# Last stage of a two-layer kernel: the value products move ahead of the score products in three slots of four, and two other steps move with them

## The chip, the cores and the metric

The kernel runs on one NeuronCore of a Trainium2 chip, all in fp32. The metric is the device time of one execution in microseconds. Engines are called as in the profile: PE is TensorE (its matmuls; PEld are its weight loads), DVE is VectorE, ACT is ScalarE, POOL is GpSimd, SP is the engine that issues most DMAs.

## What is computed

The input `x` has 16 batch elements of 256 tokens with 256 features. Four layers add to it one after another: a cross-attention, a top-2 mixture of experts, a second cross-attention, and a gated linear attention. The change is in the last one. For each of 8 heads of 64 features it computes (cut to what matters):

```
q1, k1, v  = x@Wq, x@Wk, x@Wv                  # dense part
q2         = x@Wqa@Wqb ;  k2 = softmax(x@Wka@Wkb)   # routed part
gk1, gk2   = log_sigmoid(x@Wg1a@Wg1b + b)/16, log_sigmoid(x@Wg2a@Wg2b + b)/16
S_t = diag(exp(gk_t)) S_{t-1} + k_t^T v_t ;  o_t = q_t S_t     # for (q1,k1,gk1)
o  += the same with (q2,k2,gk2), each token kept by the one expert it is routed to
o   = o * rsqrt(mean(o*o) + eps) * norm_w
o   = o * (g * sigmoid(g)),   g = x@Wga@Wgb
x  += tanh(gate) * (o @ Wo)
```

## The kernel before, in words

The kernel writes the recurrence as causal scores over all 256 tokens. With c the running sum of the log gates, `q*exp(c)` and `k*exp(-c)` are multiplied to a table tokens x tokens, masked, and applied to `v`. There are two such tables for each head, the first for the dense part and the second for the routed part. They are added before they meet `v`.

**Slots.** The last stage (`stage3_fast`, L1619) runs over 64 slots, `for p in range(last)`, with p = 4b + m: batch element b, and m = 0..3 a pair of heads. Small steps of the coming batch elements (projections, gates, routing, norms) are hung into the slots by lists (`middle`, `rest`, `late`, `behind_mask`, `by_rows`, `logs`, from L2039), each with the slot number m in which it runs. Every engine is pinned to the order of the program (`Pinned`, L42): an instruction that waits holds up all that is behind it on its engine. So the order of the calls in the loop is the order on each engine.

**The steps of a slot before**, with the names of the tiles that the profile shows:

- `masked(p - 1, 1)`: four DVE operations multiply the second scores of the slot before with the routing table `am` and with 1/denominator (`at<-sc,kden,am`); POOL then adds the result to the first scores (`at<-at,at`).
- `keys_queries(p + 1)`: the projections of the next slot's keys and queries (`kq`, PE).
- The hung-in steps. In m = 0 `lows` (`low`: small projections, copied by DVE). In m = 1 `all_gates` (the gates `sc<-lbg,low` and `z<-lbg,low`, of which ACT takes the exponential, `lg`), then the mean squares of the outputs (`ms`). In m = 2 the values (`v`, copied by ACT). In m = 3 the output projection (`proj`, added to `x` by DVE). On DVE there are also reductions of the gates (`gates`), the routing tables (`em`, `am`) and the routing itself.
- `decays(p + 1)`: running sums of the log gates as a product with a triangular matrix (`gq<-dmask,lg`, `gz<-em,lg`), and their exponentials on ACT (`ee`).
- `products(p, 0)`: the first scores (`sc<-f`). `masked(p, 0)`: one DVE operation applies the causal mask (`at<-sc,amask`).
- In m = 0 `route_logits`: `emx` and `e` on DVE, `e<-e` (an exponential) on ACT.
- `factors(p + 1)`: one DVE operation, `f<-kq,ee`.
- In m = 0 `outgates`: the output gate (`zg`, two banks); ACT takes an exponential (`eg<-zg`), and DVE a copy (`zs<-zg`).
- `summed(p)`: `values(p - 1)`, that is `o<-at,v`, and after each second slot the squares (`sq<-o`, ACT).
- `second(p + 1)`: `gq<-low,lbk` and `gz<-low,lbk` (queries and later keys of the routed part). `factors_second(p + 1)`: POOL makes `k`, DVE makes `q`.
- The list `logs`, where in m = 1 the statistics of `x` for a later norm stand: `stats(b + 2)`, two BNStats and two aggregates on DVE (`bst`, `mv`) and four small POOL operations (`rs`).
- `products(p, 1)`: the second scores (`sc<-q,k`).
- At the start of m = 0 also `shares` and `shares_end`: the softmax denominators of the routed keys (`den`, then `dens` on DVE).

**PSUM.** Of the eight banks, four are fixed (`kq`, `gq`, `gz`, `o`), two form the one tile `sc` (pool `psa`, one buffer), and two are general (pool `pss`, two buffers in turn, called by `bank(...)`). The tile `sc` holds the first scores, then the second scores, and in m = 1 a part of the gates. Each of these writers waits until the last reader of the one before is done. The general banks take `den`, `low`, `zg`, `z`, `ms`, `v` and `proj`.

**Shapes on PE.** A product with 128 rows and 128 columns fills the array. `sc`, `zg` and `gq/gz<-low` use halves of it (64 rows x 128 columns, two at a time), `o` uses 128 rows x 64 columns, `den` and `ms` 128 x 32, the gates 17 rows. An fp32 matmul shows as two passes in the trace: "x8" is four matmuls.

Of the kernel before, what the change touches and what calls it, by code (L numbers as in the profile page):

```python
# [10 lines left out]
F32 = mybir.dt.float32  # L11
# [6 lines left out]
P = 128  # L18
B, S, D = 16, 256, 256
# [7 lines left out]
def bc(ap, shape, *axes):  # L27

    for a in axes:
        ap = ap.unsqueeze(a)  # L30
    return ap.to_broadcast(list(shape))
# [42 lines left out]
def layers(ctx: ExitStack, tc: tile.TileContext, t, out, check):  # L74
# [102 lines left out]
    dve3, act3, pool3 = free = [Pinned(tc, x, False) for x in (nc.vector, nc.scalar, nc.gpsimd)]  # L177
# [371 lines left out]
    if fast:  # L549
        route = Route()  # L550
# [319 lines left out]
    weights = []  # L870
# [748 lines left out]
    def stage3_fast(early_bank):  # L1619

        with ExitStack() as sx:
# [7 lines left out]
            def bank(name):  # L1629
                return pss.tile([P, 512], F32, tag="ps", name=name) if pss else early_bank(name)  # L1630

            def tokens(i):
                return slice(i * P, (i + 1) * P)


            def matmul(*a, **k):
                tc.keep_in_program_order(nc.tensor.matmul(*a, **k))  # L1637
# [41 lines left out]
            def turn(b):  # L1679
                xnT[b] = of(b).tile([P, 2, S], F32, tag="xnT", name="xnT")  # L1680
                ps = bank("tr")
                for k in range(2):
                    for i in range(2):
                        transpose(ps[:, (2 * k + i) * P:(2 * k + i + 1) * P], xn[b][:, i, k * P:(k + 1) * P], ident)
                act3.copy(xnT[b], ps.rearrange("p (k s) -> p k s", k=2))
# [28 lines left out]
            e_, den_, z_, rl, rows, cols_ = {}, {}, {}, {}, {}, {}  # L1714
# [121 lines left out]
            def place(p):  # L1836
                b, m = p // 4, p % 4
                return b, m, slice(m * P, (m + 1) * P)
# [37 lines left out]

            def shares(b):

                ps = bank("den")
                x = e2[b].rearrange("p m (i q t) -> p (m i) q t", i=2, q=4)  # L1880
                for q in range(4):
                    matmul(ps[32 * q:32 * q + 32, :S], halves[:, 48:80], x[:, :, q, :], start=True, stop=True)
                z_[b, "den"] = ps
# [11 lines left out]
            def factors(p):  # L1895
                fk[p, 0] = w2.tile([P, 2, S], F32, tag="f0", name="f0")
                dve3.tensor_tensor(fk[p, 0], kq.pop(p).rearrange("p (w s) -> p w s", w=2), ee.pop((p, 0)),
                                        ALU.mult)
                fq[p, 0] = fk[p, 0][:, 1, :]
                fk[p, 0] = fk[p, 0][:, 0, :]  # L1900
# [9 lines left out]
            def products(p, n):  # L1910

                b, m, cols = place(p)
                q, k = fq.pop((p, n)), fk.pop((p, n))
                ps = psa.tile([P, 2, 512], F32, tag="sc", name="sc")
                for lo, hi, i in ((0, S, 0), (P, S, 1)):
                    for j in range(2):
                        r = slice(64 * j, 64 * j + 64)
                        matmul(ps[:, j, lo + i * P:hi + i * P], k[r, tokens(i)], q[r, lo:hi],
                                         start=True, stop=True)
                z_[p, n, "sc"] = ps  # L1920

            def masked(p, n):
                b, m, cols = place(p)
                ps = z_.pop((p, n, "sc"))
                a = w2.tile([P, 2, 384], F32, tag=f"at{n}", name=f"at{n}")
                if n == 0:
                    at[p] = a
                    dve3.tensor_tensor(a, ps[:, :, :384], bc(amask, [P, 2, 384], 1), ALU.mult)
                else:
                    r = rd[b][:, 2 * m:2 * m + 2, :]  # L1930
                    for lo, hi, i in ((0, S, 0), (S, 3 * P, 1)):
                        for j in range(2):
                            dve3.scalar_tensor_tensor(a[:, j, lo:hi], ps[:, j, lo:hi], r[:, i, j:j + 1],
                                                           am[b][:, lo:hi], ALU.mult, ALU.mult)
                    if p == last - 1:
                        at[p] = a
                        return
                    pool3.tensor_tensor(at[p], at[p], a, ALU.add)

            def values(p, first=True, end=True):  # L1940
                b, m, cols = place(p)
                if m % 2 == 0:
                    o[b, m // 2] = psu.tile([P, 512], F32, tag="o", name="o")
                ps, a = o[b, m // 2], at[p] if not end else at.pop(p)
                base = m % 2 * S
                for i, (lo, hi, to) in enumerate(((0, S, base), (S, 3 * P, base + P))):
                    for j in range(2):
                        h = slice((2 * m + j) * 64, (2 * m + j + 1) * 64)
                        matmul(ps[64 * j:64 * j + 64, to:base + S], v[b][:, i, h], a[:, j, lo:hi],
                                         start=first and i == 0, stop=end and i == 1)  # L1950
# [4 lines left out]
            def squares(b, mp):  # L1955
                if mp == 0:
                    u_[b] = w2.tile([P, 4, S], F32, tag="u", name="u")
                    oT[b] = u_[b]
                    sq[b] = w2.tile([P, 4, S], F32, tag="sq", name="sq")
                ps = o.pop((b, mp))  # L1960
                act3.activation(sq[b][:, 2 * mp:2 * mp + 2, :].rearrange("p m s -> p (m s)"), ps, AF.Square)
                z_[b, mp, "o"] = ps

            def gated(b, mp):
                ps = z_.pop((b, mp, "o"))
                dve3.tensor_tensor(u_[b][:, 2 * mp:2 * mp + 2, :].rearrange("p m s -> p (m s)"), ps,
                                        gw[b][:, 2 * mp:2 * mp + 2, :].rearrange("p m s -> p (m s)"), ALU.mult)
# [63 lines left out]
            def warm():  # L2031

                ps = bank("warm")
                for _ in range(2):
# [3 lines left out]
            start = {3: [(same, 1)]}  # L2038
            middle = {0: [(lows, 1)], 1: [(outgates_end, 0, 0), (all_gates, 1)], 3: [(scaled_first, 0)]}  # L2039

            rest = {0: [(bias, 2)], 1: [(route_sums, 1)], 2: [(norm_ahead, 2), (steepest, 1, 0)], 3: [(steepest, 1, 1), (weights, 1)]}
            late = {1: [(norms, -1)], 2: [(vals, 1), (turn_ahead, 2)], 3: [(project, -1)]}
            behind_mask = {0: [(route_logits, 1)]}
            by_rows = {0: [(outgates, 0)], 1: [(gates_end, 1)]}
            logs = {0: [(outgates_exp, 0, 1, act3.copy)],
                    1: [(route, 1), (stats, 2), (outgates_end, 0, 1), (gate_logs, 1, 0)],
                    2: [(gate_logs, 1, 1), (normed_out, -1, 0), (normed_out, -1, 1)]}

            def run(steps, p):
                for f, d, *a in steps.get(p % 4, ()):  # L2050
                    if 0 <= p // 4 + d < B:
                        f(p // 4 + d, *a)
# [17 lines left out]
            psa = sx.enter_context(tc.tile_pool(name="f3psa", bufs=1, space=PSUM, reuse_waits="tile"))  # L2070
            pss = sx.enter_context(tc.tile_pool(name="f3ps", bufs=2, space=PSUM, reuse_waits="tile"))
            last = 4 * B
            decays(0)
            for m in range(0, 3, 2):
                ps = bank("k2")
# [7 lines left out]
            def summed(p):  # L2083
                values(p - 1)
                if p % 2 == 0:
                    squares((p - 1) // 4, (p - 1) % 4 // 2)

            for p in range(last):
                if p == 0:
                    turn(1)  # L2090
                run(start, p)
                if p % 4 == 0:
                    shares(p // 4)
                if 0 < p:
                    masked(p - 1, 1)
                if p % 4 == 0:
                    shares_end(p // 4)
                if 1 < p and p % 2 == 1:
                    gated((p - 2) // 4, (p - 2) % 4 // 2)
                if p + 1 < last:  # L2100
                    keys_queries(p + 1)
                run(middle, p)
                run(rest, p)
                if p + 1 < last:
                    decays(p + 1)
                run(late, p)
                products(p, 0)
                masked(p, 0)
                run(behind_mask, p)
                if p + 1 < last:  # L2110
                    factors(p + 1)
                run(by_rows, p)

                inside = 0 < p and p + 1 < last
                if inside:
                    summed(p)
                if p + 1 < last:
                    second(p + 1)
                    factors_second(p + 1)
                run(logs, p)  # L2120
                products(p, 1)
                if 0 < p and not inside:
                    summed(p)

            b, p = B - 1, last - 1
            values(p, end=False)
            masked(p, 1)
            project_part(b, 0, 0)
            values(p, first=False)
# [122 lines left out]
```

## Time and profile before

| | us |
|---|---|
| three timed runs | 1804.23, 1805.36, 1807.59; median 1805.36 |
| the profiled execution | 1804.92 |
| its span in the profile | 1803.0 |
| PE busy | 1771.7 (98%) |
| DVE busy | 1168.2 (65%) |
| POOL busy | 1018.9 (57%) |
| ACT busy | 842.4 (47%) |
| granted PE clock, mean | 0.997 |

The 64 slots lie between 1221 and about 1785 us. A line of the timeline gives the start and the length in us, the engine, the line of the kernel (L1637 is the matmul helper of this stage, L50 the helper of the other engines), the operation, the tile written and the tiles read, shapes, and how many instructions were merged; in brackets stands the idle time of the engine before it and what ended it. Lines in a group list have the busy time and the mean length in ns, then the idle time before. Matmuls are pipelined: the length of one (0.38 us for a 256-column pass) is longer than the distance of two starts (0.22 us), so distances of starts are what counts on PE.

### The profile page before, as it was taken

How to read it: one execution, taken by the hardware profiler on the slowest of the kernel's cores; microseconds unless marked ns; L12 is line 12 of the kernel's file. 1: busy time of each engine (PE TensorE's matmuls, PEld its weight loads, DVE VectorE, ACT ScalarE, POOL GpSimd, SP SyncE). 2: the span in 40 equal slices, each digit the busy share in tenths (PEclk: the TensorE clock that was granted, in tenths of full speed). 3: DMA queues.
4: the chain of work that ended last, by engine and by line, in shares of the span. 5: the costliest groups of instructions: out<-in, count | busy, mean ns of one | idle time of the engine just before them, and what ended most of it. 6: DMA issues, size and time to landing. Idle time of an engine off the chain costs nothing.

```text
span 1803.0 us, 35245 instructions
## 1 busy us (share of the span) xinstructions
PE 1771.7 (98%) x13802; PEld 1227.0 (68%) x13802; DVE 1168.2 (65%) x2727; ACT 842.4 (47%) x1743; POOL 1018.9 (57%) x1002
## 2 busy tenths in 40 slices
PE   8999999999999999999999999999999999999997
PEld 5666666667666666667677866656777777777775
DVE  3345666666656656665566368886777777777774
ACT  4433444334444345344343368765455455545542
POOL 3655776576756766566751776513545455544543
PEclk9999999999999999999999999999999999999999
DMA  9800010000100010000037952200112111211210
GB/s 304 238 1 23 16 36 13 28 17 13 35 26 17 17 33 10 28 24 17 13 126 250 272 122 47 43 4 18 35 35 51 44 35 41 46 41 35 51 38 26
DMA packets 121623, 102.28 MB, mean 57 GB/s; under 512 B 53051, under 2 KB 106979, under 8 KB 120937
## 3 DMA queue, kind: packets, MB, share of 16 engines
q1 hardware_dynamic: 109161, 83.17, 16.0%
q0 software_dynamic: 12288, 16.79, 4.6%
q8 instruction: 110, 1.80, 0.4%
q14 instruction: 64, 0.52, 0.1%
HBM read 56.26 MB, written 38.44 MB: 53 GB/s over the span
## 4 chain that ended last, share of the span: by engine, by line
PE 83%; POOL 7%; DVE 5%; issue 1%; ACT 1%; DMA 1%; SPq 0%; POOLq 0%; DVEq 0%; ACTq 0%
PE o L50 12%; PE qk L50 11%; PE v L50 9%; PE sc L50 8%; PE proj L50 7%; PE kq L1637 6%; PE sc L1637 6%; PE gq L1637 4%; POOL es L50 4%; PE o L1637 3%; PE ex L50 3%; PE proj L1637 3%; PE v L1637 3%; PE gz L1637 2%; POOL rs L50 2%; PE low L1637 2%
## 5 line engine op out<-in xcount | busy, mean ns | idle before, releaser
L50 POOL TENSOR_SCALAR rs<-mv 128x2 f32<-128x2 f32 (+2 forms) x85 | 16.3, 192 | 398.3 <-DVE mv L50 393.7
L50 POOL TENSOR_TENSOR at<-at,at 128x768 f32<-128x768 f32 x63 | 114.3, 1814 | 184.0 <-DVE at L50 184.0
L50 DVE RECIPROCAL rd<-o 128x256 f32<-128x256 f32 x64 | 112.3, 1755 | 155.8 <-PE o L50 155.8
L50 ACT ACTIVATE e<-sc 128x1024 f32<-128x1024 f32 (+1 forms) x192 | 181.6, 1016 | 18.4 <-PE sc L50 18.4
L50 PE MATMUL sc<-qk 64*128 64x256 f32 (+1 forms) x1536 | 183.1, 384 | 0.5 <-DVE qk L50 0.5
L50 PE MATMUL o<-e,v 128*32 128x256 f32 (+1 forms) x3072 | 177.9, 379 | 0.0
L50 PEld LDWEIGHTS sc<-qk 64*128 64x128 f32 (+1 forms) x1536 | 132.0, 172 | 55.1 <-issue 26.8
L50 POOL TENSOR_TENSOR esum<-esum,es 128x512 f32<-128x512 f32 x128 | 163.5, 1277 | 10.0
L50 PE MATMUL qk<-kvT,wkv 128*128 128x333 f32 x512 | 164.3, 443 | 0.0
L50 POOL TENSOR_TENSOR es<-e 128x1024 f32<-128x1024 f32 x64 | 151.3, 2364 | 12.1 <-ACT e L50 9.0
L50 ACT ACTIVATE qk<-qk 128x256 f32<-128x256 f32 x128 | 48.8, 381 | 231.5 <-PE qk L50 231.5
L50 POOL TENSOR_TENSOR es<-es,e 77x1024 f32<-77x1024 f32 x64 | 150.5, 2351 | 5.0
L50 PEld LDWEIGHTS o<-e,v 128*32 128x32 f32 (+1 forms) x3072 | 99.9, 110 | 66.3
L50 PE MATMUL qk<-kvT,wq 128*128 128x256 f32 x512 | 134.6, 385 | 0.0
L50 DVE COPY qk<-qk 128x333 f32<-128x333 f32 x128 | 64.6, 505 | 94.8 <-ACT qk L50 93.3
L50 POOL DMA_INDIRECT x<-rows_out,pos x64 | 100.9, 1577 | 35.5 <-issue 16.6
L50 PEld LDWEIGHTS qk<-kvT,wq 128*128 128x128 f32 x512 | 94.3, 189 | 35.1 <-issue 9.6
L50 PEld LDWEIGHTS qk<-kvT,wkv 128*128 128x128 f32 x512 | 97.2, 190 | 30.0
L50 DVE TENSOR_TENSOR at<-sc,amask 128x768 f32<-128x768 f32 x64 | 61.3, 957 | 84.9 <-PE sc L1637 83.9
L50 PE MATMUL proj<-wo0h,oT 128*128 128x256 f32 x512 | 113.7, 380 | 0.3 <-DVE oT L50 0.3
L50 PE MATMUL v<-wkv,kvT 128*128 128x512 f32 x256 | 113.1, 595 | 0.0
L50 PEld LDWEIGHTS proj<-wo0h,oT 128*128 128x128 f32 x512 | 95.9, 190 | 13.9 <-issue 0.8
(259 smaller groups left out, 3912.5 us busy)
## 6 DMA issues: line engine op xcount, KB each, us to landing
rows<-zero SPq DMA_DIRECT2D x16, 640.0 KB
xin<-rows SPq DMA_DIRECT2D x16, 640.0 KB
r<-rms SPq DMA_DIRECT2D x30, 256.0 KB
rows_out<-y SPq DMA_DIRECT2D x16, 384.0 KB
v<-vctx SPq DMA_DIRECT2D x15, 308.0 KB
x<-in_x_dram SPq DMA_DIRECT2D x16, 256.0 KB
rows_out<-y SPq DMA_DIRECT2D x16, 256.0 KB
rows<-picks SPq DMA_DIRECT2D x16, 256.0 KB
```

The lines of the kernel that those rows point to most:

```text
L50: x = getattr(self.engine, name)(*a, **k)
L1637: tc.keep_in_program_order(nc.tensor.matmul(*a, **k))
```

## The change

Four things are moved, and no arithmetic is changed.

1. In slots with m = 0, 2, 3 (`ahead`), `factors(p + 1)` and `summed(p)`, so `o<-at,v`, run before `products(p, 0)` in place of after it. The first slot moves only `factors`, the last one nothing; m = 1 stays as it was.
2. In slots with m = 2 and 3 the second scores go to two general banks (`sc1`), in place of the tile `sc`. In exchange `den` goes from a general bank to the tile `sc`.
3. The four mask operations of the second scores run head by head, in place of block by block.
4. `stats(b + 2)` moves within m = 1 from the list `logs` to the list `rest`: before the first scores, their mask and `k`, in place of after them.

```diff
 def shares(b):
-    ps = bank("den")
+    ps = psa.tile([P, 2, 512], F32, tag="sc", name="den")[:, 0, :]
...
 def products(p, n):
-    ps = psa.tile([P, 2, 512], F32, tag="sc", name="sc")
+    if n == 1 and m > 1:
+        two = [bank("sc1"), bank("sc1")]
+    else:
+        ps = z_[p, n, "sc"] = psa.tile([P, 2, 512], F32, tag="sc", name="sc")
+        two = [ps[:, 0, :], ps[:, 1, :]]
     for lo, hi, i in ((0, S, 0), (P, S, 1)):
         for j in range(2):
             r = slice(64 * j, 64 * j + 64)
-            matmul(ps[:, j, lo + i * P:hi + i * P], k[r, tokens(i)], q[r, lo:hi],
+            matmul(two[j][:, lo + i * P:hi + i * P], k[r, tokens(i)], q[r, lo:hi],
                              start=True, stop=True)
-    z_[p, n, "sc"] = ps
+    if n == 1:
+        z_[p, n, "sc"] = two
...
 def masked(p, n):
-        for lo, hi, i in ((0, S, 0), (S, 3 * P, 1)):
-            for j in range(2):
-                dve3.scalar_tensor_tensor(a[:, j, lo:hi], ps[:, j, lo:hi], r[:, i, j:j + 1],
+        for j in range(2):
+            for lo, hi, i in ((0, S, 0), (S, 3 * P, 1)):
+                dve3.scalar_tensor_tensor(a[:, j, lo:hi], ps[j][:, lo:hi], r[:, i, j:j + 1],
                                                am[b][:, lo:hi], ALU.mult, ALU.mult)
...
-rest = {0: [(bias, 2)], 1: [(route_sums, 1)], 2: ...
+rest = {0: [(bias, 2)], 1: [(route_sums, 1), (stats, 2)], 2: ...
...
-        1: [(route, 1), (stats, 2), (outgates_end, 0, 1), (gate_logs, 1, 0)],
+        1: [(route, 1), (outgates_end, 0, 1), (gate_logs, 1, 0)],
...
     run(late, p)
+    inside = 0 < p and p + 1 < last
+    ahead = p % 4 != 1 and p + 1 < last
+    if ahead:
+        factors(p + 1)
+        if inside:
+            summed(p)
     products(p, 0)
     masked(p, 0)
     run(behind_mask, p)
-    if p + 1 < last:
+    if not ahead and p + 1 < last:
         factors(p + 1)
     run(by_rows, p)
-
-    inside = 0 < p and p + 1 < last
-    if inside:
+    if inside and not ahead:
         summed(p)
```

More of the change, by code (lines that the diff above doesn't have):

```diff
@@ L2039, in stage3_fast @@
             middle = {0: [(lows, 1)], 1: [(outgates_end, 0, 0), (all_gates, 1)], 3: [(scaled_first, 0)]}
-            rest = {0: [(bias, 2)], 1: [(route_sums, 1)], 2: [(norm_ahead, 2), (steepest, 1, 0)], 3: [(steepest, 1, 1), (weights, 1)]}
+            rest = {0: [(bias, 2)], 1: [(route_sums, 1), (stats, 2)], 2: [(norm_ahead, 2), (steepest, 1, 0)], 3: [(steepest, 1, 1), (weights, 1)]}
             late = {1: [(norms, -1)], 2: [(vals, 1), (turn_ahead, 2)], 3: [(project, -1)]}
```

## The prediction

> **What bounds the kernel now.** I read the page first, then stretches of the last stage (1221 to 1795 us) in the timeline, engine by engine.
>
> ```profile
> span 1803.0 us, 35245 instructions
> ## 1 busy us (share of the span) xinstructions
> PE 1771.7 (98%) x13802; PEld 1227.0 (68%) x13802; DVE 1168.2 (65%) x2727; ACT 842.4 (47%) x1743; POOL 1018.9 (57%) x1002
> ...
> PE 83%; POOL 7%; DVE 5%; issue 1%; ACT 1%; DMA 1%; SPq 0%; POOLq 0%; DVEq 0%; ACTq 0%
> ```
>
> TensorE (PE) is the bound. In the last stage the starts of its matmuls show how strictly: from one `kq` to the next, slots take 9.78, 8.35, 7.64 and 9.19 us, the same to 0.01 us from batch to batch with two exceptions (slots 36 and 46). A batch takes 34.96 us, and nearly all of it is issued without a pause. So little waiting is there to be removed, and the question is which chains beside PE are just as long. One is. I number slots p = 4b + m. This is p = 40 (m = 0); first PE, then VectorE (DVE), then ScalarE (ACT):
>
> ```profile
> 1586.73 0.92 PE L1637 MATMUL sc<-f 64*128 64x256 f32 x8
> ...
> 1592.46 0.70 PE L1637 MATMUL sc<-lbg,low 17*128 17x512 f32 x2
> ```
>
> ```profile
> 1587.77 0.96 DVE L50 TENSOR_TENSOR at<-sc,amask 128x768 f32<-128x768 f32 x1 [0.53 <-PE sc L1637]
> 1588.76 0.18 DVE L50 TENSOR_REDUCE emx<-rl 32x8 f32<-32x32 f32 x1
> 1588.97 0.18 DVE L50 TENSOR_TENSOR e<-rl,emx 32x32 f32<-32x32 f32 x1
> 1589.18 0.69 DVE L50 TENSOR_TENSOR f<-kq,ee 128x512 f32<-128x512 f32 x1
> 1590.07 0.69 DVE L50 COPY zs<-zg 128x512 f32<-128x512 f32 x1 [0.19 <-ACT eg L50]
> 1590.67 0.41 DVE L50 TENSOR_TENSOR q<-gq,ee 128x256 f32<-128x256 f32 x1
> 1591.00 1.38 DVE L50 SCALAR_TENSOR_TENSOR at<-sc,kden,am 128x256 f32<-128x256 f32 x4
> ```
>
> ```profile
> 1589.19 0.23 ACT L50 ACTIVATE e<-e 32x32 f32<-32x32 f32 x1 [1.58 <-DVE e L50]
> 1589.43 0.60 ACT L50 ACTIVATE eg<-zg 128x512 f32<-128x512 f32 x1
> ```
>
> Read it as a chain. The first score group `sc<-f` ends; its mask starts 1.04 us after the group's start; `e` on DVE releases `e` on ACT; that lets `eg` run; `zs` starts 0.03 us after `eg` ends; then `q`, then the second mask, which ends at 1592.39. The gate matmuls of slot p = 41 (`sc<-lbg,low`) write the same `sc` tile and start at 1592.46. PE gets there by its own work at 1592.46 too. From `sc<-f` to the gates both paths are 5.73 us long. That there is no slack is seen at p = 44, where the mask came 0.35 us later relative to its slot:
>
> ```profile
> 1623.08 0.96 DVE L50 TENSOR_TENSOR at<-sc,amask 128x768 f32<-128x768 f32 x1 [0.88 <-POOL k L50]
> ```
>
> ```profile
> 1627.76 0.70 PE L1637 MATMUL sc<-lbg,low 17*128 17x512 f32 x2 [0.27 <-DVE at L50]
> ```
>
> The gates came 0.34 us later in their slot, and PE is shown waiting for DVE. Delay on this chain is delay of the kernel.
>
> **The change, part by part.**
>
> *Values ahead of the scores.* The eight passes `o<-at,v` (128 rows x 64 columns) stand between `sc<-f` and `gq/gz<-low` (both 64 rows x 128 columns); in slots m = 0, 2, 3 they move ahead of `sc<-f` (not in the first and the last slot). Each change of the array's shape costs: `sc<-f` takes 0.85 us to the next start if `o` follows and 0.75 if the equally shaped `zg` does; the first `gq` pass after `o` takes 0.32 us, against 0.22 in slot 0, where no `o` stands before it (1239.75 to 1239.97). One stay in the 64-row shape is saved in each slot: 0.10 + 0.10 = 0.20 us. Before `o` the array comes from another shape as before, so that side stays. `o` needs the sum `at` of the slot before from GpSimd (POOL): in slot 40 it is ready at 1585.08 and `o` moves to 1586.73; in slots 2 and 3 there are about 1.5 us as well, once the statistics are out of the way. No cost.
>
> *Slots m = 2 (16 of them).* -0.20 us. The second scores go to two general banks, last used by `v`, whose second copy ends at 1605.31, 1.1 us before the scores would come (1606.42). Nothing waits.
>
> *Slots m = 3.* -0.20 us, but a wait is added: `den` moves from a general bank to the `sc` tile, so it waits for the first mask. What that takes is in the last slot, where nothing else stands between:
>
> ```profile
> 1780.68 0.92 PE L1637 MATMUL sc<-f 64*128 64x256 f32 x8
> 1782.74 0.49 PE L1637 MATMUL sc<-q,k 64*128 64x256 f32 x2 [1.13 <-DVE at L50]
> ```
>
> 2.05 us from `sc<-f` to the next writer of the tile. In slot 3 PE will have 0.75 (`sc<-f`) + 0.43 (`gq/gz` without the switch) + 0.75 (`sc<-q,k`) = 1.93 us of work, so `den` waits 0.12, and all PE work behind it (`kq`, `low`) with it. DVE is free in time: the projection's sum ends at 1579.54, `factors` takes 0.68, the mask is due about 1580.3. Bounds of this wait: 0 to 0.4 (if the masks `em`, which wait for a DMA, come late). I take 0.12.
>
> *Slots m = 0 (p = 4 to 56: 14 with the chain).* The -0.20 is still PE's, but `sc<-f` starts 0.80 us later, behind `o` (its row: 1588.45 to 1589.25). The whole chain above hangs on it. `factors` leaves the place between `e` and `zs`, but there it lay beside `e` and `eg` on ACT (it ended at 1589.87, `eg` at 1590.03), so its absence shortens nothing. At its new place it waits only for `ee` (1587.05) and is done by 1588.0, before the mask at 1588.57. So mask, `e`, `eg`, `zs`, `q` and second mask each come 0.80 later, and the gates start at 1593.26 in place of 1592.46. PE will reach them at about 1592.3 and idle 1.0 us. Queued behind them are `gq`, `gz`, `ms` and the next `sc<-f`; that one already waits for ACT to empty the gates (2.78 us after them), so nothing is caught up in m = 1. Net +0.80 us from `kq` to the gates, the 0.20 swallowed.
>
> Here a rule weighs. The Trainium skill, *PSUM — Partial Sum Buffer*, "PSUM bank collisions raise a hardware error", says that two engines must not be in one bank and quadrant at once, two readers included, and that the scheduler therefore adds a dependency between them. `eg` and `zs` read one bank, and the row has `zs` 0.03 us behind `eg`. If that were only a coincidence of order, `zs` could start straight after `e`, with `factors` gone, about 0.9 us sooner: the second mask would end where it does now and the slot would cost nothing. By the rule and the row it can't; I take +0.80.
>
> *Statistics sooner (m = 1).* Two BNStats and two aggregates, about 0.97 us of DVE (1599.51 to 1600.48), move ahead of the mask, where DVE now idles from 1593.42 to 1596.28; they fit even if held up behind POOL's 1.81 us sum. On POOL the four small `rs` steps (1.56 us) move ahead of `k`, needed a slot later. This is what frees the sum `at` of m = 1, now done at 1605.14 while the moved `o` of m = 2 wants it at 1604.43: without it 0.7 us would be lost per batch. On its own it gives nothing. Its DMAs: SP still waits for `picks` before `rows` and `cols`, and `turned` follows those; nothing moves.
>
> *Mask order and squares.* Four masks per slot either way, 1.38 us. `squares` goes ahead of `e` on ACT, which idles there 1.58 us and needs 0.59. Nothing.
>
> *The end.* In slot 63 the second scores no longer wait for the mask, only for the projection's bank (emptied at 1781.54): 1781.6 in place of 1782.74, -1.1 us, and the tail behind follows. Slots 58 to 60, after the last gates, give -0.20 - 0.08 - 0.20 = -0.5; in slot 62 the projection waits for POOL's `u` anyway.
>
> **Sum.** Per batch -0.20 - 0.20 + 0.12 + 0.80 = +0.52 us; x14 = +7.3. Less 1.1 and 0.5 at the end, and 0.3 for the accident of slot 44, which lies off the new path: +5.4 us. On the profiled execution (1804.9 us, span 1803.0) that is 1810.3. The median of the three timed runs is 1805.36, 0.4 above it; I predict 1810.6 us.
>
> **Rivals.**
> - *The chain has slack after all, and the change is faster.* If the gates are not moved by the late mask (a slack of 0.80 us or more in m = 0 would be needed), slot 0 gives -0.20 too: 14 x -0.48 = -6.7, with -1.6 at the end -8.3 us: 1797. For it: the 0.20 us per switch is plain in the rows, at three places a batch. Against it: p = 44.
> - *About half of the shift arrives*, because something of the chain is overlapped (`zs` or `q` sooner): +0.1 per batch, 1805 to 1806, no change that can be told.
> - *More waits than I see*: `den` at its upper bound (+0.3 a batch), or masks held up behind POOL steps as at p = 44 (+0.35 in m = 1, where the slack for `sc<-q,k` is only 0.14). +0.4 to 0.6 a batch: 1816 to 1819.
> - *The change does not do what it says.* Freeing the second scores from the first mask is worth nothing in the middle: waits of `sc<-q,k` for DVE sum to 1.5 us over slots 1257 to 1757 us. This is already in the sum.
>
> **How the numbers follow.** About 0.2% (3.6 us) can be told from no change. The likeliest case, 1807 to 1814, has 0.60, of which 0.08 lies below 1809. More waits 0.13, half the shift 0.12, the chain with slack 0.15. Slower: 0.52 + 0.13 = 0.65; same 0.08 + 0.12 = 0.20; faster 0.15. The range 1802 to 1818 takes in the likeliest case, the half shift and most of the added waits, and leaves out the faster rival.
>
> **What would show it.** From one `kq` to the next, the four slots of a batch are now 8.35 (m = 0), 7.64 (m = 1), 9.19 (m = 2) and 9.78 us (m = 3); by the sum they become 8.15, 8.64, 8.99 and 9.70, 35.5 in all. In m = 1 the gates should stand 1.0 us behind the end of PE's `kq`, with DVE's second mask named as what ended the wait; in m = 0 the mask should start 0.80 us later in its slot with `zs` still 0.03 us behind `eg`; in m = 3 `den` should start 2.05 us after `sc<-f`. I am wrong if the gates follow `kq` without a wait, if `zs` starts before `eg` ends, or if PE waits in m = 2.

## The result, and the profile after

The changed kernel takes 1816.98 us (median of 4 runs, 1814.86 to 1817.81), the kernel before 1805.54 us on the same chips. The ratio is 1.0066 [1.0053, 1.0079]: slower by 11.4 us; the brackets hold the 95% interval of the ratio. The profiled execution took 1814.86 us, the fastest of the four. From its page:

```profile
span 1813.1 us, 35294 instructions
## 1 busy us (share of the span) xinstructions
PE 1765.4 (97%) x13802; PEld 1227.1 (68%) x13802; DVE 1164.8 (64%) x2727; ACT 845.4 (47%) x1743; POOL 1019.9 (56%) x1002
...
PE 79%; DVE 7%; POOL 7%; ACT 3%; issue 2%; DMA 1%; SPq 0%; POOLq 0%; DVEq 0%; ACTq 0%
```

TensorE is busy 6.3 us less in a span that is 10.1 us longer: it does the same instructions and stands still more. In the chain that ended last its share falls from 83 to 79%, and VectorE's and ScalarE's rise from 5 and 1% to 7 and 3%. The list of waits, asked for PE over the fourteen full batches of the last stage, says where (waited for, us in total, times, longest us); first after, then before:

```profile
PE sc L1637 <- DVE at L50: 13.1, 14, 0.9
PE o L1637 <- POOL at L50: 1.3, 1, 1.3
PE den L1637 <- DVE at L50: 0.5, 1, 0.5
PE proj L1637 <- DVE at L50: 0.5, 2, 0.2
```

```profile
PE sc L1637 <- DVE at L50: 1.7, 3, 1.2
```

One wait a batch of 0.94 us has come, always the same: a matmul into the tile `sc` that waits for a mask on DVE. (Waits under 0.15 us are not in this list.) The timeline of PE in slot p = 40 (m = 0) shows which matmul:

```profile
1592.86 0.87 PE L1637 MATMUL o<-at,v 128*64 128x256 f32 x8
1593.66 0.92 PE L1637 MATMUL sc<-f 64*128 64x256 f32 x8
...
1596.56 1.13 PE L1637 MATMUL kq<-xnT,wk 128*128 128x256 f32 x4
1597.53 1.03 PE L1637 MATMUL kq<-xnT,wq 128*128 128x256 f32 x4
1599.49 0.70 PE L1637 MATMUL sc<-lbg,low 17*128 17x512 f32 x2 [0.94 <-DVE at L50]
```

It is the gates of slot 41. Without a wait they follow the start of `kq<-xnT,wq` by about 0.97 us; here by 1.96. The same slot on DVE, then on ACT:

```profile
1593.40 0.69 DVE L50 TENSOR_TENSOR f<-kq,ee 128x512 f32<-128x512 f32 x1
1594.70 0.96 DVE L50 TENSOR_TENSOR at<-sc,amask 128x768 f32<-128x768 f32 x1 [0.61 <-PE sc L1637]
1595.69 0.18 DVE L50 TENSOR_REDUCE emx<-rl 32x8 f32<-32x32 f32 x1
1595.90 0.18 DVE L50 TENSOR_TENSOR e<-rl,emx 32x32 f32<-32x32 f32 x1
1596.99 0.69 DVE L50 COPY zs<-zg 128x512 f32<-128x512 f32 x1 [0.91 <-ACT eg L50]
1597.72 0.42 DVE L50 TENSOR_TENSOR q<-gq,ee 128x256 f32<-128x256 f32 x1
1598.06 1.38 DVE L50 SCALAR_TENSOR_TENSOR at<-sc,kden,am 128x256 f32<-128x256 f32 x4
```

```profile
1593.77 0.60 ACT L50 ACTIVATE sq<-o 128x512 f32<-128x512 f32 x1
1596.12 0.23 ACT L50 ACTIVATE e<-e 32x32 f32<-32x32 f32 x1 [1.74 <-DVE e L50]
1596.37 0.60 ACT L50 ACTIVATE eg<-zg 128x512 f32<-128x512 f32 x1
```

The chain is the one of before, link by link, only later. DVE stands idle for 0.91 us ahead of `zs`, which starts 0.02 us after `eg` ends; the second mask ends at 1599.44, and PE goes on at 1599.49. Meanwhile the squares and the new place of the factors, both done by 1594.4, have shortened nothing.

Measured from one `kq` to the next, the slots of a batch are:

| slot | before | predicted | after |
|---|---|---|---|
| m = 0 | 8.35 | 8.15 | 8.25 |
| m = 1 (holds the gates' wait) | 7.64 | 8.64 | 8.65 |
| m = 2 | 9.19 | 8.99 | 8.99 |
| m = 3 | 9.78 | 9.70 | 9.79 |
| batch | 34.96 | 35.5 | 35.68 |

14 x 0.72 = 10.1 us, the whole difference of the spans. The other terms nearly cancel (they are in the section on the prediction).

### The profile page after: what moved, and what is told of

Same layout as the page of the kernel before. It is cut to its first block, busy times and chain, and to the rows that moved or that the text cites. A ratio compares the mean times of both kernels' runs of the same rounds, so it can differ in the third digit from the quotient of the medians.

```text
span 1813.1 us, 35294 instructions
## 1 busy us (share of the span) xinstructions
PE 1765.4 (97%) x13802; PEld 1227.1 (68%) x13802; DVE 1164.8 (64%) x2727; ACT 845.4 (47%) x1743; POOL 1019.9 (56%) x1002
## 4 chain that ended last, share of the span: by engine, by line
PE 79%; DVE 7%; POOL 7%; ACT 3%; issue 2%; DMA 1%; SPq 0%; POOLq 0%; DVEq 0%; ACTq 0%
PE o L50 12%; PE qk L50 11%; PE v L50 9%; PE sc L50 8%; PE proj L50 7%; PE sc L1637 5%; PE kq L1637 5%; POOL es L50 4%; PE ex L50 3%; PE proj L1637 3%; PE o L1637 3%; PE gq L1637 3%; PE v L1637 2%; DVE at L50 2%; POOL rs L50 2%
## 5 line engine op out<-in xcount | busy, mean ns | idle before, releaser
L50 POOL TENSOR_TENSOR at<-at,at 128x768 f32<-128x768 f32 x63 | 114.4, 1816 | 224.5 <-DVE at L50 224.5
```

What stands on the lines that cost most here:

```text
L50: x = getattr(self.engine, name)(*a, **k)
```

## The experiments

The theory: the loss is the m = 0 chain, and only there; its stiff link is that `zs` on DVE waits for `eg` on ACT, and `eg` for the routing's exponential. Rivals: the moved steps themselves (factors, statistics), the general banks or the wait of `den` cost the time; or the values ahead give nothing anywhere. Each ratio below is to the kernel before, timed in the same rounds on the same chip, with its 95% interval in brackets. Each diff is against the changed kernel, unless the text names another; `...` stands for lines left out.

**Values ahead in m = 2 and 3 only.**

```diff
-ahead = p % 4 != 1 and p + 1 < last
+ahead = p % 4 > 1 and p + 1 < last
```

> The changed kernel, with the values ahead of the first scores in slots m = 2 and 3 alone (m = 0 as before the change). Theory 1 (the loss is the chain of slot m = 0: mask, e, eg, zs, q, second mask, gates): from kq to kq 8.35 (m = 0), 7.64, 8.99, 9.79 us, the gates follow kq without a wait; a batch 34.8 us, and with the shorter last slot some 4 us less than the kernel before. Rival (the loss is den's new wait and the second scores in general banks): still 5 us or more above the kernel before.

Measured: 1804.11 us, ratio 0.9995 [0.9987, 1.0003]. The slots are 8.35, 7.65, 8.99 and 9.79. The loss is gone with the moved values of m = 0. The slots are as expected, but the 4 us did not come: the interval takes in no change at all. From the last `kq` to the end it takes 32.75 us, as in the kernel before (32.77), where 1.1 us less was expected. More on the end, and on m = 3, which gives nothing, follows below.

**Values ahead in m = 0 only.**

```diff
-ahead = p % 4 != 1 and p + 1 < last
+ahead = p % 4 == 0 and p + 1 < last
```

> The changed kernel with the values ahead in slots m = 0 alone. Theory 1: the gates come 0.91 us later in 14 batches, nothing is saved in m = 2 and 3 and den does not wait: 14 x 0.91 - 1.1 = 11 to 12 us above the kernel before, no better than the whole change. Rival: m = 0 saves its 0.20 us in each batch and den no longer waits: 2 to 4 us under the kernel before.

Measured: 1817.18 us, 1.0070 [1.0056, 1.0084]; slots 8.25, 8.65, 9.19 and 9.78. This slot alone makes the whole loss.

**No values ahead; the other parts stay.**

```diff
-ahead = p % 4 != 1 and p + 1 < last
+ahead = False
```

> The changed kernel without its first part: values and factors behind the first scores in all slots; general banks for the second scores, den in the tile sc, head by head masks and earlier statistics stay. Theory 1: slots as in the kernel before (den has 2.7 us behind sc<-f and does not wait), 1.1 us less in the last slot: 1 us under the kernel before. Rival (den, banks or statistics carry the loss): 5 to 10 us above it.

Measured: 1803.88 us, 0.9995 [0.9987, 1.0003]. All four slots are as before to 0.01 us. The second scores in other banks, the masks head by head and the statistics sooner, taken together, cost nothing and give nothing in the middle by themselves; they were not run one by one.

**The stiff link cut.** ACT's exponential of the routing goes behind `eg`, so that `eg`, and with it `zs`, no longer hangs on `e` from DVE.

```diff
-    act.activation(e, e, AF.Exp)
+def route_exp(b):
+    act.activation(e_[b], e_[b], AF.Exp)
...
-by_rows = {0: [(outgates, 0)], 1: [(gates_end, 1)]}
+by_rows = {0: [(outgates, 0), (route_exp, 1)], 1: [(gates_end, 1)]}
... (and the same step ahead of the loop, for the first batch element)
```

> The changed kernel with one step more moved: in slot m = 0 ScalarE takes the routing exponential e behind eg, the first exponential of the output gate, in place of ahead of it. All the values stay ahead. Theory 1: eg no longer hangs on the mask, zs starts right after e on VectorE, about 0.9 us sooner, and the gates come at 10.3 us after kq (11.18 in the changed kernel, 10.27 in the one before); 14 x 0.88 = 12 us less than the changed kernel, about level with the kernel before or 1 us under it. Rival (den, banks): nothing changes, 10 us or more above the kernel before.

Measured: 1802.89 us, 0.9989 [0.9981, 0.9997]: 14 us less than the changed kernel with one small step of 0.23 us moved (12.0 by the spans of the profiled executions, as expected). The same slot, p = 40, on DVE, then ACT, then PE:

```profile
1586.98 0.96 DVE L50 TENSOR_TENSOR at<-sc,amask 128x768 f32<-128x768 f32 x1 [0.61 <-PE sc L1637]
1587.97 0.18 DVE L50 TENSOR_REDUCE emx<-rl 32x8 f32<-32x32 f32 x1
1588.18 0.18 DVE L50 TENSOR_TENSOR e<-rl,emx 32x32 f32<-32x32 f32 x1
1588.41 0.69 DVE L50 COPY zs<-zg 128x512 f32<-128x512 f32 x1
1589.14 0.42 DVE L50 TENSOR_TENSOR q<-gq,ee 128x256 f32<-128x256 f32 x1
1589.48 1.38 DVE L50 SCALAR_TENSOR_TENSOR at<-sc,kden,am 128x256 f32<-128x256 f32 x4
```

```profile
1587.79 0.60 ACT L50 ACTIVATE eg<-zg 128x512 f32<-128x512 f32 x1 [1.13 <-PE zg L1637]
1588.41 0.23 ACT L50 ACTIVATE e<-e 32x32 f32<-32x32 f32 x1
```

```profile
1589.82 1.03 PE L1637 MATMUL kq<-xnT,wq 128*128 128x256 f32 x4
1590.92 0.70 PE L1637 MATMUL sc<-lbg,low 17*128 17x512 f32 x2
```

ACT's wait ahead of `eg` is now for PE's `zg` and no longer for DVE, and `zs` needs to wait no more; from the first mask's start to the second's it is 2.50 us in place of 3.36. The first mask is as late as in the changed kernel, and yet the gates come only 0.13 us behind PE's own pace. The late mask alone does not make the loss; it takes the link as well.

**The same cut in the kernel before.** Its edit is the one above, on the kernel before.

> The kernel before with one step moved: e's exponential behind eg on ScalarE in slot m = 0. It shortens the chain from the first scores to the gates by about 0.8 us, while TensorE's own way there stays 5.73 us long. Theory 1 (both ways are equally long before, TensorE is the bound): no change beyond 0.5 us. Rival (the chain already holds TensorE up before the change): up to 0.8 x 14 = 11 us faster.

Measured: 1805.39 us, 0.9999 [0.9990, 1.0008]. DVE's second mask, then PE's gates, in slot 40:

```profile
1593.26 1.38 DVE L50 SCALAR_TENSOR_TENSOR at<-sc,kden,am 128x256 f32<-128x256 f32 x4
```

```profile
1594.03 1.03 PE L1637 MATMUL kq<-xnT,wq 128*128 128x256 f32 x4
1594.99 0.70 PE L1637 MATMUL sc<-lbg,low 17*128 17x512 f32 x2
```

The mask is done at 1594.64, 0.35 us before the gates, and they come no sooner: before the change the two paths were equally long, so shortening one is worth nothing.

**Factors back behind the first mask.** The values stay ahead.

```diff
-if ahead:
-    factors(p + 1)
-    if inside:
-        summed(p)
+if ahead and inside:
+    summed(p)
...
-if not ahead and p + 1 < last:
+if p + 1 < last:
     factors(p + 1)
```

> The changed kernel with factors back behind the first mask in all slots; values stay ahead. In the changed kernel the gates are 0.91 us late in slot m = 0, 0.80 of it the later mask, and 0.11 because q on VectorE starts 0.72 us after zs, where it started 0.61 after it before. Theory A: the 0.11 comes with the place of factors (it no longer stands between e and zs): q starts 0.61 behind zs again, 1.5 us less than the changed kernel. Theory B: it comes with something else of the later mask: q stays at 0.72, no change to the changed kernel. Either way the first part keeps its loss without factors: 9 us or more above the kernel before.

Measured: 1825.1 us, 1.0107 [1.0092, 1.0123], 8 us more than the changed kernel. One thing came as theory A has it: in m = 0 the second mask starts 9.62 us after `kq`, not 9.74. I missed the total: the tile `kq` has one buffer, and PE now waits for the factors that read it. PE in a slot m = 2:

```profile
1620.32 0.82 PE L1637 MATMUL sc<-q,k 64*128 64x256 f32 x8
1621.87 1.10 PE L1637 MATMUL kq<-xnT,wk 128*128 128x256 f32 x4 [0.73 <-DVE f L50]
```

The slot is 9.79 in place of 8.99. Where the values go ahead, the mask and all that follows it come late, and the factors must leave its back. This part of the change, which I had costed at nothing, is a condition of the first.

**Statistics back behind the second scores.**

```diff
-1: [(route_sums, 1), (stats, 2)]
+1: [(route_sums, 1)]
...
-1: [(route, 1), (outgates_end, 0, 1), (gate_logs, 1, 0)]
+1: [(route, 1), (stats, 2), (outgates_end, 0, 1), (gate_logs, 1, 0)]
```

> The changed kernel with the statistics back at their old place in slot m = 1. By the prediction the sum at of m = 1 is then ready 0.7 to 0.8 us after the moved values of m = 2 want it: slot m = 2 grows from 8.99 to 9.7 or 9.8 us, 15 x 0.75 = 11 us above the changed kernel (about 1828). If the place of the statistics doesn't matter: equal to the changed kernel.

Measured: 1825.95 us, 1.0116 [1.0101, 1.0132]. PE in a slot m = 2:

```profile
1615.55 3.60 PE L1637 MATMUL v<-wv,xnT 128*128 128x512 f32 x8
1619.84 0.87 PE L1637 MATMUL o<-at,v 128*64 128x256 f32 x8 [0.69 <-POOL at L50]
```

```profile
1615.22 0.19 POOL L50 TENSOR_SCALAR rs<-mv 128x2 f32<-128x2 f32 x1 [3.75 <-DVE mv L50]
...
1617.97 1.82 POOL L50 TENSOR_TENSOR at<-at,at 128x768 f32<-128x768 f32 x1
```

The moved values wait for GpSimd's sum, which stands behind the statistics' steps there and ends at 1619.79; the slot is 9.75 in place of 8.99. The 0.7 us a batch of the prediction is 0.76.

**The cut, and values ahead in m = 0 and 2 only.** The edit of the cut, and:

```diff
-ahead = p % 4 != 1 and p + 1 < last
+ahead = p % 4 in (0, 2) and p + 1 < last
```

> The version with e's exponential behind eg, with the values ahead in slots m = 0 and 2 alone (in m = 3 as before the change). If den's wait (0.21 us) eats what m = 3 saves (0.20), and the values ahead there make late routing masks em cost more, this is equal to or up to 1.5 us faster than that version with m = 3 too: about 1801.5, 4 us under the kernel before. From kq to kq 8.25, 7.79, 8.99, 9.78. If m = 3 did save something, it is 2 to 3 us slower than that version.

Measured: 1803.44 us, 0.9986 [0.9979, 0.9992]; slots 8.25, 7.79, 8.99 and 9.78. It is no slower without the values ahead in m = 3, so these give nothing. Nor do those of m = 0, even with the cut: 8.25 + 7.79 is 0.05 more than the 8.35 + 7.64 of before.

**Values ahead in m = 2 only, and not in slot 62.** This came from comparing the ends of the kernels above.

```diff
-ahead = p % 4 != 1 and p + 1 < last
+ahead = p % 4 == 2 and p + 2 < last
```

> Values ahead of the scores only in the slots m = 2, and not in slot 62; the rest of the change stays. Theory: the array change saves 0.20 us in m = 2 and nothing elsewhere, so the four slots of a batch are 8.35, 7.64, 8.99 and 9.78 us, 34.76 in all, 0.20 less than before, 14 times: -2.8. In the changed kernel the moved values of slot 62 wait 0.64 us for GpSimd's sum, and the whole stretch from the last kq to the end is 32.87 us; with the values back it is 32.1, as in the kernel with no values ahead (before: 32.77): -0.7. In all -3.5 us, about 1802.0. Rival: the tail loses its gain to the second scores in a general bank alone; then the stretch stays near 32.8 us and the time is about 1802.7. If the slots m = 2 had gained only through their neighbours, they would stay at 9.19 and the time at about 1804.8.

Measured: 1800.78 us (8 runs), 0.9974 [0.9964, 0.9985], the fastest of all, and faster than both kernels. The slots are 8.35, 7.65, 8.99 and 9.78, as expected; the last `kq` to the end takes 32.23 us (32.1 expected, 32.87 in the changed kernel). In slot 62 of the changed kernel PE reads:

```profile
1783.71 0.87 PE L1637 MATMUL o<-at,v 128*64 128x256 f32 x8 [0.64 <-POOL at L50]
...
1787.64 1.10 PE L1637 MATMUL ms<-sq,halves 128*128 128x512 f32 x2 [1.12 <-DVE at L50]
```

The first wait goes with this edit, the second stays (0.93 us in the kernel with no values ahead): `ms` wants a general bank, and the second scores now hold one until their mask is done. Before, `ms` did not wait.

**`den` back in a general bank,** with values ahead in m = 2 and 3 but not in slot 62.

```diff
-ps = psa.tile([P, 2, 512], F32, tag="sc", name="den")[:, 0, :]
+ps = bank("den")
...
-ahead = p % 4 != 1 and p + 1 < last
+ahead = p % 4 > 1 and p + 2 < last
```

> Values ahead in the slots m = 2 and m = 3 (not in slot 62), and the denominator den back in a general bank, where it does not wait for the first mask; the rest of the change stays. Theory: the slots m = 3 gain nothing in the changed kernel because den waits 0.21 us for the mask, so without that wait they are 9.58 us in place of 9.79, den starts about 1.93 us after sc<-f, and a batch is 8.35 + 7.64 + 8.99 + 9.58 = 34.56 us: -5.6 us over 14 batches and -0.7 at the end, about 1799.2. Rival: the restart of PE behind a semaphore, not the mask, sets the place of den, and it stays near 2.14 us with the slot at 9.79: about 1802.2. If the general banks run short, because the second scores and den now both want them, a wait appears at den or behind it, and the slot is longer than 9.79.

Measured: 1817.99 us, 1.0064 [1.0051, 1.0078]. It did not tell theory and rival apart; the third case came. PE, then DVE, in a slot m = 3:

```profile
1588.70 0.82 PE L1637 MATMUL sc<-q,k 64*128 64x256 f32 x8
1590.64 0.64 PE L1637 MATMUL den<-e,halves 128*32 128x256 f32 x8 [1.11 <-DVE at L50]
```

```profile
1589.76 1.38 DVE L50 SCALAR_TENSOR_TENSOR at<-sc,kden,am 128x256 f32<-128x256 f32 x4
```

The general banks are short: `den` waits for the first head's half of the second mask (it ends at 1590.49) in place of the first mask, and the slot is 10.77 us. The move of `den` into `sc` belongs to the move of the second scores out of it.

## Why the prediction was right, and where its sizes were wrong

The direction, the place and the mechanism were right: the m = 0 chain has no slack, a mask 0.80 us late moves the gates, and the wait stands in m = 1 where it was forecast. The size was off, +11.4 us by the medians in place of +5.2. It lies in the stated range, but not in the likeliest case (1807 to 1814): it is where the rival "more waits than I see" had its 1816 to 1819. By the profiled executions, cut at the `kq` of slots 2, 58 and 61:

| term | predicted | measured |
|---|---|---|
| up to slot 2 | 0 | -0.3 |
| 14 batches, regular | +7.3 | +10.1 |
| accidents in them | -0.3 | +0.3 |
| slots 58 to 60 | -0.5 | -0.2 |
| the end | -1.1 | +0.1 |
| sum | +5.4 | +10.0 |

Of the 4.6 us that were missing, 1.5 are 0.11 a batch in m = 0, 1.3 are 0.09 a batch at `den`, 1.2 the end and 0.6 the accidents; the rest cancels. So the range held, but the sum reached only half of the loss.

*m = 2, -0.20.* Right to 0.01 us, and the runs show that the move gives it: with the values ahead the slot is 8.99, without 9.19, in every kernel in which PE does not wait there. That a change of shape is what it saves is read from the rows.

*m = 0, +0.80.* Too small by 0.11. Each step down to `zs` came later by 0.80 exactly, then `q` follows `zs` by 0.72 us, before by 0.61, so the gates come 11.18 us after `kq` in place of 10.27. "Its absence shortens nothing" was said of the factors; their absence costs 0.11: with them back behind the mask, the second mask came 0.12 sooner. What matters is the step on DVE before `zs`. Where that is the routing's `e`, which works on partitions 64 to 95 only, `q` starts 0.03 us after `zs` ends. Where it is `factors`, or the first mask as in slot 60 (which has no routing step), both on all 128 partitions, `q` starts 0.08 us before `zs` ends. This is so in all twelve profiles, wherever PE does not hold `q` up. The runs show the order that costs the 0.11, not the reason.

The saving of 0.20 was only 0.10 in the slot itself (`sc<-q,k` takes 0.85 us to `kq` in place of 0.75), which the gates' wait swallows. The other 0.10 goes into a wait that I had not looked for. In m = 0 the second scores still need the tile `sc`. Before, they came 1.05 us after the first mask's end; now they start 0.05 us after it (1595.71 after 1595.66). The loads of their weights, before and after:

```profile
1589.57 0.84 PEld L1637 LDWEIGHTS sc<-q,k 64*128 64x128 f32 x8
```

```profile
1595.71 0.73 PEld L1637 LDWEIGHTS sc<-q,k 64*128 64x128 f32 x8 [0.23 <-DVE at L50]
```

Before, the load ran 0.21 us ahead of the first pass (1589.78); now it starts with it, and that pass takes 0.32 us to the next in place of 0.22. This is the same 0.10 as at `gq` behind `o`, where the load also starts with the pass (1589.25), but here the shape of the array does not change. So the rows tie this 0.10 to weights that are not loaded ahead; a change of shape is one case of it.

The step that made me take +0.80 holds as far as it was used: `zs` waits for `eg`. In the slot above it starts 0.02 us behind `eg`, although DVE had been idle for 0.91. That the shared bank is the reason for this wait no run here tests. In the cut kernel, too, `zs` at 1588.41 is not ahead of the end of `eg`, 1588.39, though it has DVE's `e` (to 1588.36) ahead of it there.

*m = 3, -0.20 + 0.12.* The wait of `den` was sized from the last slot's 2.05 us, and is longer. PE in slot 39 of the changed kernel, then DVE:

```profile
1585.60 0.92 PE L1637 MATMUL sc<-f 64*128 64x256 f32 x8
...
1586.79 0.82 PE L1637 MATMUL sc<-q,k 64*128 64x256 f32 x8
1587.74 0.64 PE L1637 MATMUL den<-e,halves 128*32 128x256 f32 x8
```

```profile
1586.64 0.96 DVE L50 TENSOR_TENSOR at<-sc,amask 128x768 f32<-128x768 f32 x1 [0.39 <-PE sc L1637]
```

The mask starts 1.04 us after `sc<-f`, as forecast, and ends at 1587.60. `den` starts 0.14 us later, 2.14 after `sc<-f`; by PE's own work it would be 1.93. So it waits 0.21 and eats the saving whole. In other slots PE goes on 0.05 us after a mask. `den` waits for two engines (ACT made its input), which could be the other 0.09. The run meant to settle it met another wait; there too `den` starts 0.15 us after the mask that frees its bank (1590.64 after 1590.49), though ACT's input had been ready for 1.3 us. So it does not come from that one bank; its cause is not shown.

*The accidents.* Slot 44's 0.35 us did go. In its place the masks `em`, which wait for a DMA, made single slots longer by 1.5 us in all (1.0 before), and one slot early in the stage took 0.2 more. These differ from run to run (0 to 1.8 us in the other kernels).

*The end, -1.1 us.* Wrong, and by a wait I did not look for. In slot 63 the second scores follow `sc<-f` by 0.76 us in place of 2.05, -1.3, as forecast. But the projection ahead of them comes 1.67 us later after the last `kq` (8.38 in place of 6.71). I had let slot 62 off with "the projection waits for POOL's `u` anyway"; it waits for `ms`, which the two waits of slot 62 above delay. One of them is the moved values' wait for GpSimd, which the run with values ahead in m = 2 only removed; the other is the price of the general banks. I checked these banks against the use before (`v`), not against the use after.

*Slots 58 to 60.* m = 2 gave its 0.20, m = 3 nothing, as in the batches. In slot 60 the saving went into two waits that I had put at nothing. `o` starts 0.65 us behind `gz`, where `sc<-f` took 0.54: it waits for GpSimd's sum, which ends at 1770.11 (`o` starts at 1770.16). And the second scores take 0.85 us, since they start 0.05 us after the first mask, as in the other slots m = 0.

The rival "more waits than I see" named `den` first, and is part of the truth; `q` in m = 0 and `ms` at the end it did not name.

## What to carry to other kernels

A step moved ahead on the busiest engine makes all that it overtakes late: follow the overtaken step's chain through the other engines to its return, and move only where that chain has slack (here m = 2, not m = 0 or 3). When the return is tight, look on the chain for a small step that is on it only by its place in a queue: moving a 0.23 us exponential gave back 12 to 14 us in the changed kernel and nothing in the kernel before. A buffer that is moved to another pool has to be checked against the next user of that pool as well as the last.

## What the runs showed of the hardware

A matmul that waits for a mask restarts 0.05 us after the mask's end where that is all that it waits for, and `den`, with two engines to wait for, 0.14 us after it (0.15 in the kernel with `den` in a general bank). A first pass whose weights are loaded ahead takes 0.22 us to the next, and 0.32 where the load starts with it, behind a change of shape (`gq` in slot 40 before) or behind a mask (`sc<-q,k` in slot 40 after). On DVE, `q` starts 0.61 us after a `zs` of 0.69 us, so before its end, when the step ahead of `zs` was one on all partitions, and 0.72 us after it, so behind its end, when that step was `e` on partitions 64 to 95; the runs show where it does so, not why.
